# A decoder layer's last attention group: one-column layernorm work moved between engines, work pieces split differently, and other accumulator banks for the last up products

## The chip, the cores and the metric

The kernel runs on one core of a Trainium2 chip. A core has a matrix engine (TensorE, PE in the profile, its weight loads PEld), a vector engine (VectorE, DVE), an activation engine (ScalarE, ACT), a general engine (GpSimd, POOL) and an engine that mostly issues transfers (SyncE, SP). Each engine executes its own instruction stream in order. Transfers are issued by SP and by GpSimd and moved by 16 DMA engines. The metric is the device time of one execution in microseconds, as the median of several runs.

## The reference

One layer of a decoder on x of shape (8, 256, 512), all in float32: attention, a decayed running sum over the context, and a gated feed-forward network, each followed by a layernorm without weights.

```python
x = _layernorm(x + _L0_attn_ref(x, Wq, Wk, Wv, Wo, Wdown, Wup))      # 16 heads of 32
x = _layernorm(x + _L0_xattn_ref(x, ctx_2048, ctx_2048, decay))       # r = d*r + k*v, out = q*r
x = _layernorm(x + _L0_ffn_ref(x, gate_cp, up_cp, down_cp))           # silu(gate)*up, 512 -> 2048 -> 512
return x
```

The three weight matrices of the feed-forward network are spline interpolations of a few thousand control points; the second layernorm sees values of a large range, since its input is x plus x times a running sum.

## The kernel before, in words

The 2048 tokens are four groups (g, 512 tokens) of two sequences each (n = 0 to 7, 256 tokens). PSUM, the matrix engine's accumulator memory, has eight banks: four in the pool `ps_big` and four in `ps_mm`. Every instruction keeps the order in which the Python program writes it, on its engine: the wrapper `Ordered` (line 299) is the helper whose line 308 nearly all rows of the profile carry, so rows are told apart by the names of their tiles.

**Attention loop** (from line 854). There are 32 passes, `s` = 0 to 31, eight to a group: two sequences times four quads of four heads. At the start of pass `s` TensorE makes the scores of pass `s + 1` into the four banks of `ps_big` (`sc`). For each head of the next pass VectorE takes a row maximum (`nmax`) and ScalarE two exponentials (`e`), which frees the head's bank; for each head of this pass TensorE transposes `e` (`tr_e`), an engine copies it out of PSUM (`eT`), and TensorE weights the values with it (`av`). In an odd quad VectorE makes reciprocals of the sums (`rec`) and a copy spread over 512 columns (`wide`, function `divide`), which TensorE transposes (`tr_rec`).

Between these go pieces of other work. Line 836 gives the last group's: for each pass two strings, the first done ahead of the fourth head's transpose, the second behind the fourth head's exponentials. Before each piece in a string, `slot()` advances every open chain by one stage. A piece "o" is two of the four matmuls of an output product (`output`, bank `ps_o`; with the last one VectorE adds `x_t`, the residual rows that `load_rows` fetched); "s" is nothing but the slot; "i" is one of eight pieces of `inputs(b)`, which prepares feed-forward block b. The first four of these transpose a column chunk of `x2` (`tr_x`), copy it to `x2T` and write it to DRAM (`xd`, by a GpSimd transfer issued with the next piece, the fourth with the fifth); the other four are matmuls (`ps_mom`) whose results `mom` go to DRAM (`md`, GpSimd transfers). Windows of `xd` and rows of `md` are read back into `xg` by SP's transfers, which wait for those writes. In the last group `inputs(0)` and `inputs(1)` are made this way.

**Chains.** `norms` runs, a stage per slot, the first layernorm (`norm_plain`), the transpose of the running sum (`tr_r`), `h2`, and the second layernorm, `norm_wide` (lines 381 to 414). Its stages: `nm` and the largest magnitude `mx` on VectorE; then five one-column operations (`mx` limited below by 1, its reciprocal `c`, `nmc`, `ce`, `t`) on VectorE; then ScalarE's square of the row with its sum `ss`, which uses `c` and `nmc`; then `va`, `tt` and `ok` on VectorE with the power `rs` on GpSimd between them; then `rc` and the scaled row, into `x2`, on GpSimd. `recur(n)` fetches a sequence's context, squares it on GpSimd (`r`, 128x1024) and scans it on VectorE.

**Feed-forward blocks** (from line 1115), four of 512 tokens. In each, `gate_up(b, j)` runs for j = 0 to 7: two gate products into two banks of `ps_mm` (`pg`), two up products into two banks of `ps_big` (`pu`), ScalarE's silu (`sg`), VectorE's product (`inter`), and SP's transfer of it, re-sorted, into `nat`. Then `exact(b, t)` for t = 0 to 15 accumulates eight matmul instructions each into four banks of `ps_big` (`y`), which are taken at t = 0; behind t = 0, in blocks 1 to 3, the block before is transposed into four banks of `ps_mm` (`tr_y`). At t = 7 the sums over `nat` are made (`ps_s`), copied and sent by GpSimd's transfers to `fin`, which the last y products of the block (`finish`) read. Behind the gate and up products of a block SP also reads the next block's `xg` and, with the chains, writes `out`.

Of the kernel before, what the change touches and what calls it, by code (L numbers as in the profile page):

```python
# [13 lines left out]
ALU = mybir.AluOpType  # L14
# [3 lines left out]
P = 128  # L18
B, T, D = 8, 256, 512
NH, DH = 16, 32  # L20
# [4 lines left out]
EPS = 1e-5  # L25
# [4 lines left out]
NTILE = INTER // P  # L30
# [285 lines left out]
def decoder_kernel(ctx: ExitStack, tc: tile.TileContext, x, xT, ctxT, wq, wkT, wvT, woT, wdownT, wup, decay, up_taps, down_taps, mom_f, sum_f, out, plan):  # L316
    nc = tc.nc
# [9 lines left out]
    make_identity(nc, ident)  # L327
    neghalf = const.tile([P, 4], F32, name="neghalf")
    nc.gpsimd.memset(neghalf, -0.5)
    x2 = const.tile([P, NT // P, D], F32, name="x2")  # L330


# [10 lines left out]
    early = first.enter_context(tc.tile_pool(name="early", bufs=1, side="right"))  # L343

    nc = Ordered(tc)
    units, chains = [], []

    def slot():

# [31 lines left out]
    def norm_wide(h, s, o):  # L381

        nm = small.tile([P, 1], F32, tag="nm", name="nm")
        nc.vector.tensor_scalar(nm, s, -1.0 / D, None, ALU.mult)
        mx = small.tile([P, 1], F32, tag="mx", name="mx")
        nc.vector.tensor_reduce(mx, h, AX.X, ALU.max, apply_absolute_value=True)
        yield
        nc.vector.tensor_scalar(mx, mx, 1.0, None, ALU.max)  # L390
        c = small.tile([P, 1], F32, tag="c", name="c")
        nc.vector.reciprocal(c, mx)
        nmc = small.tile([P, 1], F32, tag="nmc", name="nmc")
        nc.vector.tensor_tensor(nmc, nm, c, ALU.mult)
        ce = small.tile([P, 1], F32, tag="ce", name="ce")
        nc.vector.tensor_scalar(ce, c, c, EPS, ALU.mult, ALU.mult)
        t = small.tile([P, 1], F32, tag="t", name="t")
        nc.vector.tensor_scalar(t, mx, 2.0**-70, None, ALU.mult)
        yield
        ss = small.tile([P, 1], F32, tag="ss", name="ss")  # L400
        nc.scalar.activation(o, h, AF.Square, bias=nmc, scale=c, accum_out=ss)
        yield
        va = small.tile([P, 1], F32, tag="va", name="va")
        nc.vector.tensor_scalar(va, ss, 1.0 / D, ce, ALU.mult, ALU.add)
        rs = small.tile([P, 1], F32, tag="rs", name="rs")
        nc.gpsimd.tensor_tensor(rs, va, neghalf[:, 0:1], ALU.pow)
        tt = small.tile([P, 1], F32, tag="tt", name="tt")
        nc.vector.tensor_scalar(tt, t, t, ss, ALU.mult, ALU.mult)
        ok = small.tile([P, 1], F32, tag="ok", name="ok")
        nc.vector.tensor_scalar(ok, tt, F32_MAX * 2.0**-140, c, ALU.is_le, ALU.mult)  # L410
        yield
        rc = small.tile([P, 1], F32, tag="rc", name="rc")
        nc.gpsimd.tensor_tensor(rc, rs, ok, ALU.mult)
        nc.gpsimd.tensor_scalar(o, h, nm, rc, ALU.add, ALU.mult)
# [200 lines left out]
    def load_rows(n):  # L615
        xs[n] = []
        for qc in range(2):
            x_t = rows.tile([P, D], F32, tag="row", name="x_t")
            r0 = (n * 2 + qc) * P
            nc.sync.dma_start(out=x_t, in_=x[r0 : r0 + P, :])  # L620
            xs[n].append(x_t)
# [118 lines left out]
    def open_inputs():  # L740
        pool = ctx.enter_context(tc.tile_pool(name="inputs", bufs=1, side="left"))
        ffn["pool"] = pool
        ffn["mom"] = mid.enter_context(tc.tile_pool(name="mom", bufs=1, side="right"))
        ffn["mf"] = pool.tile([P, DC, 2, K2], F32, name="mf")
        nc.sync.dma_start(out=ffn["mf"], in_=mom_f)
# [20 lines left out]
    def inputs(b):  # L766

        pool, mf = ffn["pool"], ffn["mf"]
        xt = pool.tile([P, DC, GT], F32, tag="x2T", name="x2T")
        xd = dram.tile([4 * SPAN, GT], F32, tag="xd", name="xd")  # L770
        md = dram.tile([1, 20 * NTILE, GT], F32, tag="md", name="md")
        xg = pool.tile([P, NTILE // 2, GT], F32, tag="xg", name="xg", bufs=2)
        xgs[b] = xg

        def to_dram(c):
            nc.gpsimd.dma_start(out=xd[c : 4 * (P - 1 - c) + c + 1 : 4, :], in_=xt[c:, c, :])
            if c:
                row = 4 * (SPAN - c) + c - 1
                nc.sync.dma_start(out=xd[row : row + 4 * c - 3 : 4, :], in_=xt[:c, c, :])

        for c in range(DC):
            if c and b < 2:
                to_dram(c - 1)
            tr = ps_mm.tile([P, GT], F32, tag="mm", name="tr_x2")
            for t in range(TC):
                nc.tensor.transpose(tr[:, t * P : (t + 1) * P], x2[:, b * TC + t, c * P : (c + 1) * P], ident)
            (nc.vector.tensor_copy if c % 2 or b < 2 else nc.scalar.copy)(xt[:, c, :], tr)
            if b > 1:
                to_dram(c)
            yield  # L790
        if b < 2:
            to_dram(DC - 1)
        if b > 1:
            reads.append(lambda: windows(xd, xt, xg))
        else:
            windows(xd, xt, xg)
        mo = ffn["mom"].tile([P, ND, GT], F32, tag="fin", name="mom")
        ps = {}
        for c in range(DC):
            for s in (c, c + 1):  # L800
                if s // 2 not in ps:
                    ps[s // 2] = ps_mm.tile([P, GT], F32, tag="mm", name="ps_mom")
                at = slice(s % 2 * K2, (s % 2 + 1) * K2)
                nc.tensor.matmul(
                    ps[s // 2][at, :],
                    lhsT=mf[:, c, s - c, :],
                    rhs=xt[:, c, :],
                    start=(s == c + 1 or c == 0),
                    stop=(s == c or c == DC - 1),
                )  # L810
            if c == 1:
                nc.vector.tensor_copy(mo[:, 0, :], ps[0])
            if c == DC - 1:
                nc.vector.tensor_copy(mo[:, 1, :], ps[1])
                nc.scalar.copy(mo[:K2, 2, :], ps[2][:K2, :])
                nc.gpsimd.dma_start(out=md[:, : 2 * P].rearrange("h (c p) t -> (h p) c t", p=P), in_=mo[:, :2, :])
                nc.gpsimd.dma_start(out=md[0, 2 * P :], in_=mo[:K2, 2, :])
                if b > 1:
                    reads.append(lambda: moments(md, xg))
                else:  # L820
                    moments(md, xg)
            yield
# [10 lines left out]
            ("7k", "3k o o"), ("4k", "1v 2v"), ("6v", "o o 5v"), ("7v", "3v 4v"),  # L833
        ),
    ]
    FILLS = [FILLS[0], FILLS[1], FILLS[1], [("i i", "o o"), ("i i", "s s"), ("i i", "i i"), ("s s", "o o")] * 2]
    outs, ins = [], []

    def fed(g, items, first):
# [14 lines left out]
    for s, (g, bb, quad) in enumerate(steps):  # L854
        n = g * 2 + bb
        feeding = g + 1 < NG
        if quad == 0 and bb == 0:
            if feeding:
                qkvs[g + 1] = group_tiles(g + 1)
                b_now = b_next  # L860
                t_sums = token_sums(b_now, nc.gpsimd, 3 * (g > 1))
                next(t_sums)
                if g < 2:
                    for _ in t_sums:
                        pass
                chains.append(t_sums)
            else:
                first.close()
                open_inputs()
                ins += [inputs(0), inputs(1)]  # L870
        if quad == 0 and n:
            load_rows(n - 1)
            outs += [output(n - 1, qc) for qc in range(2)]
        if n and quad == ((2, 1)[bb] if feeding else 1 + bb):
            chains.append(recur(n))
# [12 lines left out]
        def divide():  # L888
            rec = small.tile([P, 2, 8], F32, tag="rec", name="rec")
            nc.vector.reciprocal(rec, sums[n][:, :, quad // 2 * 8 : quad // 2 * 8 + 8])  # L890
            wide = att.tile([P, 2, 8, DH], F32, tag="wide", name="wide")
            nc.vector.tensor_copy(wide, rec.unsqueeze(3).to_broadcast([P, 2, 8, DH]))
            return wide

        if quad % 2:
# [80 lines left out]
    nc.scalar.activation(neghalf[:, 3:4], neghalf[:, 2:3], AF.Silu)  # L976
    for _ in weights:
        pass
    mid.close()
    load_rows(NG * 2 - 1)  # L980
    units += [["o", output(NG * 2 - 1, qc), DC] for qc in range(2)]
# [9 lines left out]
    def gate_up(b, j):  # L991

        pgs, pus = [], []
        for w, pool, tag, to in ((wg, ps_mm, "mm", pgs), (wu, ps_big, "big", pus)):
            for h in range(2):
                at = slice(h * K2, (h + 1) * K2)
                ps = pool.tile([P, GT], F32, tag=tag, name="pg" if w is wg else "pu")
                nc.tensor.matmul(ps, lhsT=w[at, j * P : (j + 1) * P], rhs=xgs[b][at, j, :], start=True, stop=True)
                to.append(ps)
        for h in range(2):  # L1000
            sg = work.tile([P, GT], F32, tag="sg", name="sg")
            nc.scalar.activation(sg, pgs[h], AF.Silu)
            inter = work.tile([P, GT], F32, tag="inter", name="inter", bufs=NTILE)
            nc.vector.tensor_tensor(inter, pus[h], sg, ALU.mult)
            inters[b, 2 * j + h] = inter
# [196 lines left out]
```

## Time and profile before

| | |
|---|---|
| median of 3 runs | 582.72 us (582.32 to 583.15) |
| the profiled execution | 582.0 us, of which its span is 580.2 us |
| mean granted TensorE clock | 0.993 |
| last attention group (passes 24 to 31) | 308.1 to 380.0 us of the span |
| feed-forward blocks 0, 1, 2, 3 begin (first gate product) | 380.0, 430.0, 478.7, 525.8 us |

| window of the span, 20 us each | PE busy | DVE busy | ACT busy | POOL busy | DMA share |
|---|---|---|---|---|---|
| 320 to 340 | 17.21 | 16.62 | 13.96 | 7.36 | 0.34 |
| 340 to 360 | 18.74 | 14.21 | 13.47 | 4.46 | 0.58 |
| 360 to 380 | 18.48 | 16.81 | 11.90 | 9.52 | 0.61 |
| 440 to 460 | 20.00 | 11.69 | 9.00 | 4.55 | 0.99 |

The profile gives the busy time of each engine, groups of instructions with their mean time, the order in time, and a chain of waits: the work that ended last, followed back at each step to what released it. A row in the order of time reads: start, duration, engine, line, operation, result and inputs, count, and in brackets the time that the engine stood idle before it and what ended that. "x16" on a matrix row counts instructions; a float32 matmul is two.

### The profile page before, as it was taken

Reading aid. Unit: us, or ns where it says so; the run is one execution under the profiler, and the core shown is the slowest. Engines: PE = TensorE matmul, PEld = TensorE weight load, DVE = VectorE, ACT = ScalarE, POOL = GpSimd, SP = SyncE. Lnnn points to the kernel's source line nnn. Section 1 sums busy time; section 2 is a strip of 40 time slices with the busy share of each in tenths; the row PEclk is TensorE's granted clock in tenths of the full one; section 3 lists DMA queues with packets and bytes.
Section 4 is the critical chain, followed back from the end, with each engine's and each line's share of the span. In section 5 each row is a group of like instructions: output and inputs, shape, how many; then the busy total and the mean of one; then the engine's idle time right before and its main releaser. Section 6 shows DMA issues by size and latency. Waiting matters only on the chain.

```text
span 580.2 us, 10416 instructions
## 1 busy us (share of the span) xinstructions
PE 557.7 (96%) x3591; PEld 340.5 (59%) x3591; DVE 342.5 (59%) x742; ACT 273.8 (47%) x821; POOL 283.6 (49%) x583
## 2 busy tenths in 40 slices
PE   9999999999999999999999899899999999999993
PEld 4786777666766776767776455444343444434442
DVE  1336656586686586576587778875436415605615
ACT  0204665556564646654655667663234215305312
POOL 0446368689756648756554413313560362261263
PEclk9999999999999999999999999999999999999997
DMA  8404134333415224325223165689329959985921
GB/s 296 148 0 164 48 111 139 107 109 93 128 41 165 70 73 164 109 64 160 73 73 128 42 148 142 180 169 216 107 88 234 204 174 240 203 233 132 229 101 72
DMA packets 41699, 77.99 MB, mean 134 GB/s; under 512 B 5952, under 2 KB 10448, under 8 KB 41648
## 3 DMA queue, kind: packets, MB, share of 16 engines
q1 hardware_dynamic: 34576, 62.75, 41.5%
q0 software_dynamic: 6064, 13.41, 7.1%
q10 hardware_dynamic: 1008, 1.18, 0.7%
q8 instruction: 28, 0.46, 0.3%
q14 instruction: 23, 0.19, 0.1%
HBM read 45.22 MB, written 11.12 MB: 97 GB/s over the span
## 4 chain that ended last, share of the span: by engine, by line
PE 78%; DVE 8%; DMA 5%; ACT 4%; issue 3%; POOL 1%; SPq 0%; POOLq 0%; DVEq 0%; ACTq 0%
PE y L308 10%; PE ps_k L308 9%; PE ps_q L308 8%; PE ps_o L308 8%; PE ps_v L308 7%; PE tr_e L308 6%; PE pg L308 5%; PE ps_s L308 5%; PE pu L308 5%; PE sc L308 5%; PE av L308 4%; ACT e L308 2%; DMA fin<-sum 2%; DVE nmax L308 2%; DMA x_t<-in_x 1%
## 5 line engine op out<-in xcount | busy, mean ns | idle before, releaser
L308 ACT ACTIVATE e<-sc,nmax 128x256 f32<-128x256 f32 x256 | 120.1, 481 | 94.8 <-DVE nmax L308 94.7
L308 DVE TENSOR_REDUCE nmax<-sc 128x2 f32<-128x512 f32 x128 | 85.1, 682 | 25.9 <-PE sc L308 24.3
L308 POOL TENSOR_TENSOR taps<-taps 128x256 f32<-128x256 f32 (+1 forms) x144 | 86.6, 601 | 13.9 <-DMA taps<-in_down_taps 8.1
L308 PE MATMUL tr_e<-ident,e 128*128 128x128 f32 x512 | 68.4, 276 | 3.1 <-DVE x2T L308 0.9
L308 PEld LDWEIGHTS tr_e<-ident,e 128*128 128x128 f32 x512 | 57.2, 140 | 17.0 <-issue 8.0
L308 PE MATMUL y<-inter,wd 32*128 32x512 f32 x512 | 63.3, 599 | 0.0
L308 PE MATMUL ps_o<-w_o,yT 128*128 128x512 f32 x128 | 58.9, 599 | 1.1 <-DVE q_g L308 0.7
L308 ACT COPY eT<-tr_e 128x512 f32<-128x512 f32 x88 | 51.9, 590 | 17.0 <-PE tr_e L308 17.0
L308 ACT ACTIVATION_READ_ACCUMULATOR e<-sc,nmax 128x1 f32 x256 | 53.4, 209 | 0.0
L308 DVE TENSOR_TENSOR inter<-pu,sg 128x512 f32<-128x512 f32 x64 | 41.2, 686 | 18.7 <-PE pu L308 10.6
L308 POOL TENSOR_SCALAR va<-ss 128x1 f32<-128x1 f32 x32 | 6.3, 198 | 81.3 <-ACT tr_y L308 47.7
L308 ACT ACTIVATE sg<-pg 128x512 f32<-128x512 f32 x64 | 37.2, 597 | 18.5 <-PE pg L308 18.2
L308 PEld LDWEIGHTS y<-inter,wd 32*128 32x128 f32 x512 | 26.6, 184 | 32.4 <-issue 27.4
L308 POOL TENSOR_TENSOR rs<-va,neghalf 128x1 f32<-128x1 f32 x48 | 28.0, 583 | 35.7 <-DVE va L308 33.0
L308 PE MATMUL sc<-k_g,q_g 32*128 32x256 f32 x512 | 40.5, 402 | 0.8 <-ACT e L308 0.4
L308 PEld LDWEIGHTS ps_o<-w_o,yT 128*128 128x128 f32 x128 | 23.0, 190 | 24.8 <-issue 21.0
L308 PE MATMUL av<-eT,v_g 128*32 128x256 f32 x512 | 35.1, 385 | 0.5 <-ACT eT L308 0.5
L308 PEld LDWEIGHTS sc<-k_g,q_g 32*128 32x128 f32 x512 | 25.0, 184 | 16.9 <-issue 11.8
L308 PE MATMUL pg<-xg,wg 64*128 64x512 f32 x128 | 33.4, 599 | 0.0
L308 PE MATMUL pu<-xg,wu 64*128 64x512 f32 x128 | 32.8, 589 | 0.0
L308 POOL COPY x2p<-x 128x4 f32<-128x4 f32 (+4 forms) x144 | 32.7, 278 | 0.0
L308 DVE TENSOR_TENSOR q_g<-ps_q,q_g 128x512 f32<-128x512 f32 x28 | 18.9, 687 | 23.1 <-PE ps_q L308 20.3
(159 smaller groups left out, 915.6 us busy)
## 6 DMA issues: line engine op xcount, KB each, us to landing
nat<-inter SPq DMA_DIRECT2D x64, 256.0 KB
taps<-in_down_taps SPq DMA_DIRECT2D x40, 256.0 KB
taps<-in_up_taps SPq DMA_DIRECT2D x16, 384.0 KB
xg<-xd SPq DMA_DIRECT2D x8, 616.0 KB
r<-in_ctxT SPq DMA_DIRECT2D x8, 512.0 KB
x_t<-in_x SPq DMA_DIRECT2D x16, 256.0 KB
fin<-sum POOLq DMA_DIRECT2D x16, 256.0 KB, 4.8
out<-h SPq DMA_DIRECT2D x16, 256.0 KB
```

What stands on the lines that cost most here:

```text
L308: return lambda *a, **k: self.tc.keep_in_program_order(f(*a, **k))
```

## The change

In the last group and until the attention loop's end a flag `calm` is set. While it is set, the five one-column operations and `va`, `tt` and `ok` of `norm_wide` are issued on GpSimd instead of VectorE; the reciprocal becomes a power of -1, for which a column of constants is filled at the start. `wide` is copied by GpSimd as well. In `inputs(0)` and `inputs(1)` the copy of the fourth chunk to `x2T` is ScalarE's instead of VectorE's. The pieces are split differently around the fourth head: in the second and sixth pass of the last group one of two "i" goes behind it, and in the fourth and eighth pass one of two "o" goes ahead of it. The rows for sequence 6 are fetched at the start of pass 27 instead of 28. In feed-forward blocks 1 to 3 the last pair of up products goes into banks of `ps_mm`, which the gate products use.

```diff
+    nc.gpsimd.memset(neghalf[:, 1:2], -1.0)
...
-    units, chains = [], []
+    units, chains, calm = [], [], [False]
...
-        nc.vector.tensor_scalar(mx, mx, 1.0, None, ALU.max)
+        v = nc.gpsimd if calm[0] else nc.vector
+        v.tensor_scalar(mx, mx, 1.0, None, ALU.max)
         c = small.tile([P, 1], F32, tag="c", name="c")
-        nc.vector.reciprocal(c, mx)
+        if calm[0]:
+            v.tensor_tensor(c, mx, neghalf[:, 1:2], ALU.pow)
+        else:
+            v.reciprocal(c, mx)
...
-        nc.vector.tensor_tensor(nmc, nm, c, ALU.mult)
+        v.tensor_tensor(nmc, nm, c, ALU.mult)
...
-        nc.vector.tensor_scalar(ce, c, c, EPS, ALU.mult, ALU.mult)
+        v.tensor_scalar(ce, c, c, EPS, ALU.mult, ALU.mult)
...
-        nc.vector.tensor_scalar(t, mx, 2.0**-70, None, ALU.mult)
+        v.tensor_scalar(t, mx, 2.0**-70, None, ALU.mult)
...
+        v = nc.gpsimd if calm[0] else nc.vector
         va = small.tile([P, 1], F32, tag="va", name="va")
-        nc.vector.tensor_scalar(va, ss, 1.0 / D, ce, ALU.mult, ALU.add)
+        v.tensor_scalar(va, ss, 1.0 / D, ce, ALU.mult, ALU.add)
...
-        nc.vector.tensor_scalar(tt, t, t, ss, ALU.mult, ALU.mult)
+        v.tensor_scalar(tt, t, t, ss, ALU.mult, ALU.mult)
...
-        nc.vector.tensor_scalar(ok, tt, F32_MAX * 2.0**-140, c, ALU.is_le, ALU.mult)
+        v.tensor_scalar(ok, tt, F32_MAX * 2.0**-140, c, ALU.is_le, ALU.mult)
...
-            (nc.vector.tensor_copy if c % 2 or b < 2 else nc.scalar.copy)(xt[:, c, :], tr)
+            (nc.vector.tensor_copy if (c < 3 if b < 2 else c % 2) else nc.scalar.copy)(xt[:, c, :], tr)
...
-    FILLS = [FILLS[0], FILLS[1], FILLS[1], [("i i", "o o"), ("i i", "s s"), ("i i", "i i"), ("s s", "o o")] * 2]
+    FILLS = [FILLS[0], FILLS[1], FILLS[1], [("i i", "o o"), ("i", "i s s"), ("i i", "i i"), ("s o", "s o")] * 2]
...
+                calm[0] = True
                 ins += [inputs(0), inputs(1)]
+        if n and quad == 0 and s < 28 or s == 27:
+            load_rows(n if s == 27 else n - 1)
         if quad == 0 and n:
-            load_rows(n - 1)
...
-            nc.vector.tensor_copy(wide, rec.unsqueeze(3).to_broadcast([P, 2, 8, DH]))
+            (nc.gpsimd if calm[0] else nc.vector).tensor_copy(wide, rec.unsqueeze(3).to_broadcast([P, 2, 8, DH]))
...
+    calm[0] = False
     mid.close()
...
-        for w, pool, tag, to in ((wg, ps_mm, "mm", pgs), (wu, ps_big, "big", pus)):
+        up = (ps_mm, "mm") if b and j == NTILE // 2 - 1 else (ps_big, "big")
+        for w, pool, tag, to in ((wg, ps_mm, "mm", pgs), (wu, *up, pus)):
```

## The prediction

> **What bounds the kernel now.** I read the page first: TensorE is busy in nearly every slice, so only work or waits in front of TensorE count.
>
> ```profile
> PE 557.7 (96%) x3591; PEld 340.5 (59%) x3591; DVE 342.5 (59%) x742; ACT 273.8 (47%) x821; POOL 283.6 (49%) x583
> ```
>
> Next, the timeline of the last group, 308.1 to 380.0 us. I number its eight loop passes 24 to 31; a pass begins with the score matmuls (sc) of the next one: 308.13, 317.67, 325.66, 335.92, 345.04, 354.26, 361.90, and 371.97 for the last, which has none. VectorE is the busiest engine beside TensorE (60.2 of 76 us from 308 to 384, in the table of windows), and it queues the one-column work in front of the maxima that ScalarE's exponentials wait for. Three times in passes 25 to 30 it even stands still for ScalarE's square:
>
> ```profile
> 323.49 0.21 DVE L308 TENSOR_SCALAR va<-ss,ce 128x1 f32<-128x1 f32 x1 [0.60 <-ACT x L308]
> ...
> 342.60 0.21 DVE L308 TENSOR_SCALAR va<-ss,ce 128x1 f32<-128x1 f32 x1 [1.26 <-ACT x L308]
> ...
> 368.87 0.21 DVE L308 TENSOR_SCALAR va<-ss,ce 128x1 f32<-128x1 f32 x1 [1.88 <-ACT x L308]
> ```
>
> Third, the chain of waits over that stretch. Half of it is no engine at all: a transfer waits for a transfer, and VectorE for the last.
>
> ```profile
> 339.38 6.23 DMA md<-mom
> ...
> 347.44 7.54 DMA x_t<-in_x
> ...
> 355.11 0.33 DVE h L308
> ```
>
> Last, the same chain in feed-forward block 1; blocks 2 and 3 look alike. The first eight y matmuls take 2.55 us where eight take 1.07 in block 0: they need the banks of the last up products. Later TensorE waits for the sums to come back by DMA.
>
> ```profile
> 446.92 0.86 PE pu L308 x4
> 447.78 2.55 PE y L308 x8
> ...
> 458.45 7.04 PE ps_s L308 x32
> ...
> 466.50 6.70 DMA fin<-sum
> ...
> 473.34 3.67 PE y L308 x8
> ```
>
> **The change, part by part: the attention stretch.** Four second layernorms pass through it. Each takes mx, c, nmc, ce, t off VectorE (336.44 to 337.14: 0.7 us) and va, tt, ok (308.07 to 308.71: 0.65 us). Four copies to wide (0.426 each) and two of eight x2T copies (0.68) leave it too, and the three waits above go (3.7 us). That is 4x1.35 + 1.7 + 1.4 + 3.7 = 12.2 us of VectorE time, but little of it is TensorE's time, so I go pass by pass.
>
> Costs on GpSimd: a 128x1 operation there takes 0.19 to 0.21 us (va 0.198, rc 0.214), the power 0.56 (rs). The first five cost 4x0.2 + 0.56 + gaps = 1.6 us, va, rs, tt, ok 1.4 us. wide is not shown on GpSimd: its ends are 0.32 (copy of 128x80) and 1.27 (two-input 128x512); I take 0.85, near the one-input 128x512 at 0.77 to 0.82. [...]
>
> *Pass 24*: nothing. *Pass 25*: only one x2T copy stands before the third maximum, no wide, no va. The fourth maximum is done at 324.0 instead of 325.92. ScalarE now bounds: square to 323.35, eT 0.6, four exponentials 1.82: 325.8 instead of 327.08. Gain 1.3. The ScalarE copy of the fourth x2T column (0.586) falls after them, into 1.8 us of idle. *Pass 26*: TensorE works back to back (328.40 to 335.92), the 1.3 stays; VectorE, full from 328 on, drops 0.7 more, so its second mom copy ends 2.0 earlier (336.4). *Pass 27*: TensorE waits there until 338.38 for that copy and until 339.58 for an eT; the first half of the output product (1.73 us) fills this, delays the fourth transpose, but its eT stands behind ScalarE's square anyway. Exponentials end near 343.0, TensorE's work at 343.4 (now 345.04, then stalled): the next transposes start 2.4 earlier. *Pass 28*: VectorE waits for x_t. Moving load_rows saves nothing by itself: on SP's queue no other instruction lies between the end of pass 26 and the start of pass 28, so x_t stays behind xg<-md, which waits for md. md starts 2.0 earlier with mom, but GpSimd's longer queue (wide, then va, tt, ok ahead of r*r, 1.89 us) sends the last xd at 330.3 instead of 329.50, and xg<-xd shares the DMA engines with md. I take x_t 1.6 earlier (ends 0 and 2.0): the gain falls to 1.6. *Pass 29*: as 25, without square and va: 0.8 more, 2.4. *Pass 30*: back to back again; the x2T copy on ScalarE delays a bank by 0.4, the 0.53 us wait for h goes: 2.5. *Pass 31*: of waits of 0.56, 0.27 and what surrounds them (the 16 transposes take 3.24 us, 1.75 of them work) the half product fills about 0.9: 3.4 us at the first gate product.
>
> Covers. The squares need nmc from GpSimd: it is ready 4.7 us before in pass 25, 4 in 27, 2 in 30, and about 1.2 late in 31, where only eT of the last head is queued behind the square, 1.5 us before its use. If the cover of 27 or 30 went, two exponential pairs behind the square would wait and each microsecond would show. wide is needed by tr_rec, 1 to 2 us later in 25 and 27, level with it in 29 and 31: 0.5 us at most there.
>
> **What comes of it in block 0.** ps_s begins at 410.52 and needs the last nat at 411.4; DMA traffic dies off by 410.0, at about 212 GB/s without a break before. So 1.4 us is slack. The stream starts when SP passes md of block 1 (378.38). There GpSimd's queue is the tightest: va to ok, rc, the 0.77 us scaling, r*r, the five, two md issues; I put md 2.4 earlier on issue but, with xg<-xd 1.6 later beside it, 1.3 earlier on landing (ends 0 and 2.4). So 1.4 + 1.3 = 2.7 of the 3.4 us pass. Ends 1.4 and 3.4.
>
> **The seams.** The last up products now wait for the silu of the pair before: done at 446.42, needed at 446.76: no wait, 0.3 us to spare (upper end 0.3 each). The four y banks are free at 447.44 against 447.71: 1.48 us goes (2.55 less 1.07). tr_y wants banks at 448.8 to 450.1; silu and inter free them at 447.5 to 449.16. In block 3 this reaches the end, but nat traffic stops at 549.8 and would be needed just then: I take 1.3 (ends 0.9, 1.48). In blocks 1 and 2 TensorE then waits for fin: its four transfers land 7.9 us after issue, against 2.3 in blocks 0 and 3, because 2.4 MB on SP's queue (xg, out) are ahead until about 468.4; 1 MB at 250 GB/s after that gives 472.6, and it landed at 473.2. Nothing of that moves with the seam. I take 0.2 each (ends 0, 1.48). [...] The added memset (0.1 us) lies on idle GpSimd time at the start.
>
> **Sum.** 2.7 + 0.2 + 0.2 + 1.3 = 4.4 us. The profiled execution took 582.0 (span 580.2 and 1.8 around it): 577.6. It lies 0.7 below the median 582.72, so 578.3 as a median.
>
> **Rivals.**
> *Transfers hold it* (0.18): x_t and md land when they do now. Then pass 29 starts afresh, block 0 lets only its 1.4 us slack through, and block 3 gives 1.3: 2.7 us, 580.0. For it: the chain above; against it: md follows mom.
> *The seam's wait only moves* (0.08), to tr_y or to the up products: 2.7 us of attention alone, 580.0. Against it: the bank times above.
> *Nothing holds it* (0.13): 3.4 + 0.4 (x_t at its other end) + 3x1.48 = 8.2, 574.5. Against it: nat and fin backlogs.
> *Slower: GpSimd's queue becomes the bound* (0.15). Place: passes 30 and 31, where r*r, eight one-column operations, the md issues and wide stand in one queue, and ScalarE's square and SP's md wait on it. It decides once md of block 1 is issued later than 374.36 + 1.4 + 1.3 = 377.1, the slack and block 3's gain being used up; each microsecond beyond costs one. If each of the 14 new operations in 29 to 31 took 0.56 as the power does, that is 14x0.36 = 5.0 us more than I reckon; on top of 372.0, with the square that much later once (1.6), md is issued at 378.6, 1.5 past the point: 584.2. Against it: 128x1 rows of 0.2, and GpSimd at 9.5 of 20 us from 360 to 380.
>
> **Numbers.** My forecast has 0.46 and its own range 576.5 to 579.7 (block 0 at its ends, 1.4 and 3.4, and 1 us more for fin below). A measurement of this kernel can tell about 0.2% (1.2 us) from no change: faster is below 581.5, slower above 583.9. Of the two 580.0 cases (0.26) I leave 0.09 within that bound, because their waits can also grow. Faster 0.46 + 0.13 + 0.17 = 0.76, same 0.09, slower 0.15. The range 574.5 to 583.5 leaves out most of the slower case and the lower half of the case without a hold.
>
> **What would show it.** Right: DVE's waits for ACT x gone between 317 and 380, exponentials of pass 25 ending near 325.8, y x8 at 1.1 us in blocks 1 to 3, and a longer wait of y for fin in blocks 1 and 2 (about 2 us where now 0.79 and 1.00). The first gate product near 376.6; ps_s of block 0 interrupted or late against it. Wrong: ACT waiting for POOL nmc in passes 27 or 30, PE waiting for wide, x_t landing at 355 or later, tr_y or pu waiting for banks. The forecast fails as a whole if md of block 1 is issued later than now.

## The result, and the profile after

| | before | after |
|---|---|---|
| median, runs side by side | 582.93 us (582.32 to 584.05) | 589.64 us (588.41 to 590.32) |
| ratio after to before, 95% interval | | 1.0111 (1.0086 to 1.0135) |
| the profiled execution, its span | 582.0, 580.2 us | 588.4, 586.6 us |
| mean granted TensorE clock | 0.993 | 0.985 |
| first gate product of blocks 0, 1, 2, 3 | 380.0, 430.0, 478.7, 525.8 us | 381.9, 438.1, 486.6, 532.4 us |

The change costs 6.7 us; 578.3 was forecast. Executions of one kernel spread by some 6 us (the kernel before took 582.14 to 588.07 us in one series of 25), so smaller differences below are read from the intervals and from places in the traces. The two traces also start the last group 0.39 us apart (second pass at 317.67 before, 317.28 after); where I say "aligned", that is taken out.

The page of the kernel after, engine totals and the granted clock by slices:

```profile
PE 556.5 (95%) x3591; PEld 343.2 (59%) x3591; DVE 334.5 (57%) x704; ACT 274.2 (47%) x823; POOL 297.0 (51%) x620
...
PEclk9999999999999999999999997999899999999997
```

VectorE lost 8 us of work and GpSimd got 13.4 more. New is a TensorE clock that falls in two places, slices 25 (352 to 367 us) and 29 (411 to 425 us).

The chain of waits of the kernel after (start, duration, what):

```profile
337.82 8.80 DMA md<-mom
...
348.46 8.53 DMA x_t<-in_x
...
379.11 5.92 DMA md<-mom
...
408.40 9.11 DMA nat<-inter
...
417.75 7.92 PE ps_s L308 x28
```

Against the chain before, md of block 1 and nat of block 0 are new in it (and, behind these lines, nat of block 3). The order in time of the kernel after, where these transfers hold the engines:

```profile
357.12 0.69 DVE L308 SCALAR_TENSOR_TENSOR h<-ps_o,x_t 128x512 f32<-128x512 f32 x1 [7.42 <-DMA x_t<-in_x]
...
357.87 1.11 PE L308 MATMUL tr_e<-ident,e 128*128 128x128 f32 x4 [3.96 <-DVE h L308]
...
385.34 1.09 ACT L308 ACTIVATE sg<-pg 128x512 f32<-128x512 f32 x2 [2.20 <-DMA md<-mom]
...
417.75 7.92 PE L308 MATMUL ps_s<-nat,sf 128*64 128x512 f32 x28 [3.16 <-DMA nat<-inter]
```

VectorE waits 7.42 us for x_t (2.56 before), TensorE stands still for 3.96, and then four transposes take 1.11 us where they took 0.60 to 0.66. The first silu waits 2.20 us for md; I take it that `sg` lies in memory that `mom` held until its transfer was done. The sums of block 0 wait for nat, and 28 of their instructions take 7.92 us (32 took 7.02 before). The table of windows of the kernel after shows why both are slow. A row gives the window and its length, the busy time of PE, PEld, DVE, ACT and POOL with the number of instructions, and then the granted clock, the DMA share and GB/s:

```profile
350.00:355.00 5.00, 3.91 (x42) 2.00 (x40) 0.00 (x0) 1.89 (x7) 0.76 (x1) 1.00 0.83 181
355.00:360.00 5.00, 2.04 (x9) 1.64 (x10) 2.88 (x6) 1.02 (x4) 0.00 (x0) 0.70 0.17 55
360.00:365.00 5.00, 5.00 (x41) 3.98 (x43) 3.63 (x10) 4.66 (x17) 2.19 (x5) 0.62 0.48 131
...
418.00:421.00 3.00, 3.00 (x10) 1.07 (x8) 0.00 (x0) 0.58 (x1) 0.68 (x1) 0.57 0.00 0
```

With each of the two waits the clock is granted at half (0.50): from 357.0 (before the wait ends) to 363.8, and from 418.5 to 421.9 us, read in steps of 0.2 us.

Where the waits come from is on the queues. GpSimd's order in time, after:

```profile
321.44 0.61 POOL L308 COPY wide<-rec 128x512 f32<-128x512 f32 x1 [3.72 <-DVE nm L308]
...
323.25 0.26 POOL L308 TENSOR_SCALAR va<-ss,ce 128x1 f32<-128x1 f32 x1 [0.60 <-ACT x L308]
...
329.51 1.21 POOL L308 TENSOR_SCALAR x<-h,nm,rs 128x512 f32<-128x512 f32 x1
330.67 0.62 POOL L308 DMA_DIRECT2D xd<-x2T  x1
...
340.61 0.26 POOL L308 TENSOR_SCALAR va<-ss,ce 128x1 f32<-128x1 f32 x1 [1.13 <-ACT x L308]
...
367.92 0.63 POOL L308 DMA_DIRECT2D xd<-x2T  x1
```

The last row is from pass 30; before, that column stood here:

```profile
362.04 0.62 POOL L308 DMA_DIRECT2D xd<-x2T  x1
```

The wait of `va` for ScalarE's square has not gone with the move; it stands on GpSimd now, 0.60, 1.13 and in pass 30 2.46 us, and there transfers are queued behind it. The last column of block 0 is sent at 330.67 (329.50 before), that of block 1 at 367.92 (362.04). SP's order in time, after, shows what follows:

```profile
333.56 1.53 SPq L308 DMA_DIRECT2D xg<-xd  x4
346.69 1.73 SPq L308 DMA_DIRECT2D xg<-md  x2
348.46 0.96 SPq L308 DMA_DIRECT2D x_t<-in_x  x2
...
370.82 1.54 SPq L308 DMA_DIRECT2D xg<-xd  x4
385.10 1.57 SPq L308 DMA_DIRECT2D xg<-md  x2
...
388.27 12.04 SPq L308 DMA_DIRECT2D nat<-inter  x9
```

Before, these six stood at 332.37, 345.68, 347.44, 365.11, 378.38 and 382.84; the first two:

```profile
332.37 1.53 SPq L308 DMA_DIRECT2D xg<-xd  x4
345.68 1.72 SPq L308 DMA_DIRECT2D xg<-md  x2
```

`xg<-md` waits until md has landed (9.4 us behind its issue, after). GpSimd issues md of block 0 earlier than before (336.96 against 338.62), yet it lands later: about 13 us behind the windows xg<-xd in both kernels. The traces of the runs below agree: 12.7 us (late_rows) to 14.6 us (late_norm_dve) in block 0, whether md was issued 3.3 us (late_b1) or 7.8 us (best_c) behind the windows. x_t waits behind md on SP's queue, and so do `sf` (the constants of the sums) and nat in block 0.

Aligned ledger: the transposes of pass 28 begin 2.5 us earlier than before, pass 30 3.1 us later (x_t, half clock), the first gate product 2.3 later, block 1 8.5 later (nat, half clock); the seams (the passages from a block's last up products to its first y products) and the rest of blocks 1, 2 and 3 give back 0.22, 1.31 and 0.33. At the last products (`ps_c`) that is 6.6 us. The half clock alone I estimate at 4.4 of them: six groups of four transposes at about 1.06 instead of 0.60 (2.7), and 7.92 against the 6.23 us that the same 28 instructions take at full clock in runs below (1.7).

The seam in block 1, chain of the kernel after:

```profile
455.00 0.86 PE pu L308 x4
455.86 1.07 PE y L308 x8
...
473.10 7.96 DMA fin<-sum
```

The 2.55 us are 1.07, as forecast, and the sums come back 7.96 us after their issue, so most of it is waited again: y waits 2.06 us for fin (0.79 before).

### The profile page after: what moved, and what is told of

Same layout as the page of the kernel before. It is cut to its first block, busy times and chain, and to the rows that moved or that the text cites. A ratio compares the mean times of both kernels' runs of the same rounds, so it can differ in the third digit from the quotient of the medians.

```text
span 586.6 us, 10419 instructions
## 1 busy us (share of the span) xinstructions
PE 556.5 (95%) x3591; PEld 343.2 (59%) x3591; DVE 334.5 (57%) x704; ACT 274.2 (47%) x823; POOL 297.0 (51%) x620
## 3 DMA queue, kind: packets, MB, share of 16 engines
q10 hardware_dynamic: 1008, 1.18, 0.6%
## 4 chain that ended last, share of the span: by engine, by line
PE 77%; DMA 10%; DVE 6%; ACT 3%; issue 2%; POOL 1%; SPq 0%; POOLq 0%; ACTq 0%; DVEq 0%
PE ps_k L308 9%; PE ps_q L308 8%; PE ps_v L308 8%; PE tr_e L308 7%; PE ps_o L308 7%; PE y L308 7%; PE sc L308 5%; PE ps_s L308 5%; PE pg L308 5%; PE av L308 5%; PE pu L308 4%; DMA nat<-inter 3%; DMA fin<-sum 3%; DMA md<-mom 3%; ACT e L308 2%; PE ps_mom L308 2%
## 5 line engine op out<-in xcount | busy, mean ns | idle before, releaser
L308 PE MATMUL y<-inter,wd 32*128 32x512 f32 x512 | 58.9, 599 | 0.0
L308 PEld LDWEIGHTS y<-inter,wd 32*128 32x128 f32 x512 | 24.9, 184 | 29.7 <-issue 27.4
L308 PE MATMUL sc<-k_g,q_g 32*128 32x256 f32 x512 | 38.9, 401 | 0.4 <-ACT e L308 0.2
L308 PE MATMUL pg<-xg,wg 64*128 64x512 f32 x128 | 36.4, 600 | 0.3 <-ACT sg L308 0.3
L308 PE MATMUL pu<-xg,wu 64*128 64x512 f32 x128 | 35.7, 589 | 0.0
L308 PE MATMUL ps_s<-nat,sf 128*64 128x512 f32 x128 | 30.5, 626 | 4.1 <-DMA nat<-inter 4.1
```

The costliest lines, as they stand in the source:

```text
L308: return lambda *a, **k: self.tc.keep_in_program_order(f(*a, **k))
```

## The experiments

Theory 1 was: GpSimd's queue sends the last column late, with it go the windows, md, x_t, the first silu and nat. Theory 2: the results that GpSimd now makes (nmc, wide) are late for ScalarE and TensorE. Theory 3: the seam's banks. All runs are timed beside the kernel before; a table stands at the end.

**Each half of the change alone.** seam_only is the kernel before with

```diff
-        for w, pool, tag, to in ((wg, ps_mm, "mm", pgs), (wu, ps_big, "big", pus)):
+        up = (ps_mm, "mm") if b and j == NTILE // 2 - 1 else (ps_big, "big")
+        for w, pool, tag, to in ((wg, ps_mm, "mm", pgs), (wu, *up, pus)):
```

> The kernel before, with nothing but the last up products of blocks 1 to 3 in the banks of the gate products. Theory 1 (the whole loss comes from the attention stretch: GpSimd's queue sends the last x2T column later, and with it the transfers that follow): the three waits of y at the seam go, 2.55 to 1.07 us each, block 2 (its carry of 1.3 in the changed kernel) keeps most of it and blocks 1 and 3 give theirs back to the sums and the rows that come by DMA: 581.0 to 582.5, no more than 0.3 above the kernel before. Theory 3 (the banks cost more than they bring, because up products now wait for the silu of the pair before): 584 or more, and 'pu' waiting for ACT.

attn_only is the changed kernel with these lines as before.

> The changed kernel with the last up products left in their old banks, so the attention stretch alone is changed. Theory 1: the first block 1 gate product stands 8 us later than in the kernel before, as in the changed kernel (438.14 against 430.06), and the end 7 to 8 us later than before: 590 to 591. Theory 3 (the banks are what costs): 583 to 584.

582.07 and 590.61 us: the whole loss lies in the attention stretch. Theory 3 falls.

**The column sent at once, and x_t ahead of md.** xd_now, on the changed kernel:

```diff
-            if c and b < 2:
-                to_dram(c - 1)
...
-            if b > 1:
-                to_dram(c)
+            to_dram(c)
             yield
-        if b < 2:
-            to_dram(DC - 1)
```

> The changed kernel, but each x2T column of inputs 0 and 1 is sent as soon as it is copied, not with the next piece. Theory 1: SP issues xg<-xd of block 0 at about 330 instead of 333.56 and that of block 1 3 to 5 us earlier than 370.82; md lands 13 us behind each, so the wait of VectorE for x_t in pass 28 falls from 7.4 us to about 4, and the first silu and the nat stream come 3 to 5 us earlier: 584 to 586 in all. Theory 2 (GpSimd's late results, nmc and wide, hold ScalarE and TensorE, and the transfers only follow): 589 to 590. Theory 3 (the banks): 589 to 590.

rows_26:

```diff
-        if n and quad == 0 and s < 28 or s == 27:
-            load_rows(n if s == 27 else n - 1)
+        if n and quad == 0 and s < 28 or s == 26:
+            load_rows(n if s == 26 else n - 1)
```

> The changed kernel, but load_rows(6) is issued at the start of pass 26, not 27, so on SP's queue x_t stands ahead of xg<-md of block 0, not behind it. Theory 1: the 7.4 us wait of VectorE for x_t in pass 28 is gone, pass 29 starts 4 us or more earlier; the second half of the delay (xg<-xd of block 1, then md, then nat) shrinks by less, since it follows GpSimd's queue: 584 to 587. Theory 2 (nmc and wide late) and theory 3 (banks): 589 to 590.

584.79 and 585.07 us, some 5 us better each, as theory 1 had it; theory 2 gave 589 to 590. In xd_now the last columns go at 327.16 and 362.68, xg<-xd at 330.03 and 366.48, x_t is waited for 1.90 us and nat starts at 382.60. This profiled execution, 581.19 us, is the shortest of ten; the four above 586 us had a mean clock of 0.987 to 0.990, this one 0.993. In rows_26 that wait is gone and the first gate product comes 3.6 us earlier than before (aligned), but nat still starts at 383.78 (382.9 aligned, against 382.84 before), and in the profiled execution TensorE waits 3.41 us for it, with the half clock behind.

**Which part makes the queue late.** Each run undoes one part of the changed kernel: norm_dve issues the eight one-column operations on VectorE again, wide_dve the copy to `wide`, pieces_old has the old strings and the fourth column's copy on VectorE.

```diff
-        v = nc.gpsimd if calm[0] else nc.vector
+        v = nc.vector
```

> The changed kernel, with the eight one-column operations of each second layernorm back on VectorE; wide stays on GpSimd, the pieces stay split. Theory 1a (these operations are what makes GpSimd's queue send the last column late): in block 0's turn va, tt, ok (0.3 each with gaps 1.2 us) leave the queue, in block 1's turn mx to t (1.9 us): last xd near 329.5 and 364.5 instead of 330.67 and 367.92, x_t 1.2 us earlier, nat 3 us earlier: 585 to 587. Theory 1b (wide on GpSimd does it) or 1c (the split of the pieces does it): 589 to 590.

```diff
-            (nc.gpsimd if calm[0] else nc.vector).tensor_copy(wide, rec.unsqueeze(3).to_broadcast([P, 2, 8, DH]))
+            nc.vector.tensor_copy(wide, rec.unsqueeze(3).to_broadcast([P, 2, 8, DH]))
```

> The changed kernel, with the copy to wide back on VectorE alone. Theory 1a or 1c: 588.5 to 590, since wide lies 0.6 us ahead of an xd that is followed by a wait for ScalarE anyway. Theory 1b: 584 to 586, last xd of block 1 at 365 or earlier.

```diff
-    FILLS = [FILLS[0], FILLS[1], FILLS[1], [("i i", "o o"), ("i", "i s s"), ("i i", "i i"), ("s o", "s o")] * 2]
+    FILLS = [FILLS[0], FILLS[1], FILLS[1], [("i i", "o o"), ("i i", "s s"), ("i i", "i i"), ("s s", "o o")] * 2]
```

> The changed kernel, with the pieces ordered as before the change and the fourth x2T column copied by VectorE. Theory 1c (the later place of the second piece and of the copy is what sends the columns late): 584 to 586, last xd at 329.5 and 364 or earlier. Theory 1a or 1b: the last xd stays where it is within 0.5 us, since r*r and the layernorm's operations still stand before it, and TensorE loses the gain of pass 25: 589 to 591.

585.58, 588.45 and 588.28 us. The one-column operations are the main part: with them on VectorE the last columns go at 330.03 and 364.40, and x_t is waited for 4.41 us instead of 7.42. From norm_dve:

```profile
355.48 0.69 DVE L308 SCALAR_TENSOR_TENSOR h<-ps_o,x_t 128x512 f32<-128x512 f32 x1 [4.41 <-DMA x_t<-in_x]
...
364.40 0.62 POOL L308 DMA_DIRECT2D xd<-x2T  x1
```

wide does little. The pieces lie between what theories 1a and 1c gave: the last column of block 1 goes 2 us earlier with the old order (365.88 against 367.92), so they have a small share.

**The kernel before with the rows early** (the edit of rows_26 on the kernel before):

> The kernel before, with nothing but load_rows(6) at the start of pass 26, ahead of the transfers that wait for md. Theory 1 (the rows stand behind md on SP's queue in both kernels): VectorE's wait of 2.56 us for x_t in pass 28 goes, pass 30 and with it the last xd of block 1, md and nat come up to 2.5 us earlier: 580 to 581.5. If the place on SP's queue is not what holds x_t: 582.5 to 583.5, wait still there.

584.13 us, ratio 1.0014 (0.9992 to 1.0035): a miss for both. The wait for x_t is gone, and pass 30 begins at 361.81 against 361.90 us. The 2.56 us that VectorE stood still before were covered: TensorE waits for an x2T copy in both, 0.95 us before and 1.18 here, and goes on at the same time:

```profile
359.44 0.66 PE L308 MATMUL tr_e<-ident,e 128*128 128x128 f32 x4 [1.18 <-DVE x2T L308]
```

The tail of a chain of waits is no proof that its link costs time.

**The half clock.** warm puts three products without use ahead of the sums of block 0 in the changed kernel:

```diff
+                if b == 0:
+                    warm = ps_mm.tile([P, GT], F32, tag="mm", name="warm")
+                    for _ in range(3):
+                        nc.tensor.matmul(warm, lhsT=wd[:, :P], rhs=inters[b, t], start=True, stop=True)
```

> The changed kernel, with three extra matrix products (2.8 us by y's 0.46 us an instruction; the result is not used) on TensorE just ahead of the sums of block 0, where it waits 3.16 us for the last nat and then runs its 28 sum instructions at a granted clock near 0.5 (7.92 us instead of 6.23). Theory 4 (a TensorE wait of some 2.4 us and more makes the clock fall to half for some 3.3 us, which adds 1.7 us behind the wait): the wait shrinks under 1 us, the sums take 6.23, and 1.0 to 1.7 us go: 588 to 588.6. Rival (the sums are slow because nat arrives piece by piece): still 7.9 us, no gain, 589.6 or more.

Order in time of warm:

```profile
412.84 2.84 PE L308 MATMUL warm<-inter,wd 128*128 128x512 f32 x6
415.62 1.08 PE L308 MATMUL ps_s<-nat,sf 128*64 128x512 f32 x4
417.26 6.23 PE L308 MATMUL ps_s<-nat,sf 128*64 128x512 f32 x28 [0.56 <-DMA nat<-inter]
```

588.09 us: more work on TensorE, and by the medians 1.5 us less (ratio 1.0059 against 1.0111; the two intervals touch). The same 28 instructions take 6.23 us when TensorE did not stand still ahead of them, though they too wait for the last nat, 0.56 us, and start only 0.5 us earlier than in the kernel after (417.26 against 417.75). Not all of the gain is theirs: in this trace the half clock of pass 28 also lasts 3.4 us instead of 6.8, and pass 30 begins 0.9 us earlier (aligned). The 2.4 us of theory 4 is no bound on which these traces agree: the half clock followed a wait of 2.35 us in rows_26 and not one of 2.87 us in wide_dve.

**Transfers off GpSimd's queue.** best_a is the changed kernel with the edit of rows_26 and

```diff
-            nc.gpsimd.dma_start(out=xd[c : 4 * (P - 1 - c) + c + 1 : 4, :], in_=xt[c:, c, :])
+            (nc.gpsimd if b > 1 else nc.sync).dma_start(out=xd[c : 4 * (P - 1 - c) + c + 1 : 4, :], in_=xt[c:, c, :])
...
-                if b > 1:
+                if b:
                     reads.append(lambda: moments(md, xg))
```

and each column sent with its own piece. best_b has the one-column operations on VectorE besides; best_c is the kernel before with the seam and this diff.

> The changed kernel with its transfers taken off GpSimd's queue and off each other: both parts of each x2T column of blocks 0 and 1 are issued by SP right behind the copy, load_rows(6) comes in pass 26, and xg<-md of block 1 is issued behind block 0's nat. Theory 1: xg<-xd of block 0 at 330 or earlier, no wait for x_t, pass 30 at 360 to 361, first nat at 380 to 381.5 instead of 388.27, block 0's sums 2 us earlier than in the kernel before, and the seam's 1: 578.5 to 580.5. Theory 2 (nmc and wide late hold the engines): 583 or more, since their waits in pass 31 (1.86 and 1.5 us) stay.

> As the run before, with the one-column operations of the second layernorm back on VectorE (wide on GpSimd, pieces split). Theory 1: the transfers no longer depend on GpSimd's queue, so these operations matter little now: within 1 us of the run before, 578.5 to 581. Theory 2: 2 us or more better than the run before, ACT's wait for nmc in pass 31 being gone.

> The kernel before, with the last up products in the gate products' banks, both parts of each x2T column of blocks 0 and 1 issued by SP right behind the copy, and xg<-md of block 1 behind block 0's nat; nothing of the layernorm, wide, pieces or rows is moved. Theory 1: xg<-xd of block 0 at 328 to 330, of block 1 at 361 to 363, first nat near 381.5, and 1 to 1.5 us from block 0 and 1 from the seams: 580 to 581.5; what best_a has beyond it is what the moved work brings once the transfers don't wait for it.

580.59, 582.0 and 581.9 us, with ratios of 0.9957, 0.9957 and 0.9961: all faster than before, but each 0.1 to 1 us above its expected range. On SP's queue the last column of block 1 lies right behind r (512 KB), and the windows of block 1 are issued at 367.74 in best_a and 369.02 in best_c (365.11 before), 5.2 and 7.2 us behind that column (3.1 before); md lands behind them: SP passes it, with `sf`, at 382.23 and 384.81, and TensorE waits 1.63 and 1.52 us for the first silu (0.35 in the kernel after). A hold was moved, not taken away. The one-column operations make no difference between best_a and best_b that these runs can tell.

**Both holds apart.** Two holds are left: on SP's queue x_t stands behind md, and md lands behind the windows. Blocks 2 and 3 read their windows and rows behind nat. late_b1 lets block 1 do so too, on the changed kernel:

```diff
-        if b > 1:
+        if b:
             reads.append(lambda: windows(xd, xt, xg))
...
-                if b > 1:
+                if b:
                     reads.append(lambda: moments(md, xg))
```

> The changed kernel, but block 1's windows (xg<-xd) and rows (xg<-md) are read behind block 0's nat transfers, as blocks 2 and 3 do it, instead of in passes 30 and 31. If the windows in flight are what holds md: md of block 1 lands 5 to 7 us behind its own issue (near 384 or earlier), the first silu waits 1 us or less for it, the first nat goes at 383.5 to 384.5 instead of 388.27, and since fewer bytes share the DMA engines with nat the sums of block 0 wait less than 1 us: 584 to 585.5. The wait for x_t in pass 28 (7.4 us) and the half clock behind it stay. If md is late for itself: nat at 387 or later, 588 to 589.

late_rows has this and the edit of rows_26.

> As the run before, and load_rows(6) in pass 26, so both holds are gone. If the two holds carry the whole loss, the forecast of the attention stretch and of the seam comes true: first gate product 3.4 us earlier than in the kernel before (near 376.6 on its time axis), first nat at 379 to 380, no wait of the sums over 1 us, block 1 begins 3 us or more earlier than in the kernel before, the seams give another 1: 577 to 579. If something else in the moved work costs time: 581 or more.

late_before is the kernel before with the seam and this diff.

> The kernel before with the seam's banks and with block 1's windows and rows read behind block 0's nat; nothing of the layernorm, wide, pieces or rows moved. Its first gate product stays at 380.0 and its first silu waits for nothing, so nat starts at 382.5 to 383 as before and has fewer bytes beside it: block 0 gives 0 to 0.5 us, the seams 1: 581 to 582. What late_rows has beyond it is what the moved work brings when no transfer holds it, about 3 us; if it has less than 1 us more, the moved work brings nothing.

584.65 and 578.05 us lie in their ranges, 582.09 lies 0.09 above its own. In late_b1 md is issued at 379.10, and `sf`, which waits for it on SP's queue, goes at 383.25, 4.1 us later instead of 6.8:

```profile
379.10 1.42 POOL L308 DMA_DIRECT2D md<-mom  x2
...
383.25 0.33 SPq L308 DMA_DIRECT2D sf<-in_sum_f  x1
```

nat starts at 385.57, 1 us later than expected, and the sums are not interrupted; the wait for x_t (7.81 us) and the half clock behind it remain. late_rows, the chain of waits:

```profile
376.91 1.06 PE pg L308 x4
...
407.39 7.02 PE ps_s L308 x32
...
426.86 1.06 PE pg L308 x4
...
461.88 8.28 DMA fin<-sum
...
536.64 9.55 DMA nat<-inter
...
560.29 2.87 PE ps_c L308 x12
```

The first gate product and block 1 come 3.7 us earlier than before (aligned by 0.48), the last products (`ps_c`) 4.8. The clock stays at full. late_rows is 0.97% faster than the kernel before (0.9903, 0.9874 to 0.9932); late_before 0.36%. The difference, 0.6% or some 4 us, is what the moved work brings once no transfer waits for it. The early rows are counted with it; alone, on the kernel before, they brought nothing (before_rows_26). The waits of theory 2 in pass 31 are still there in late_rows (1.86 us for nmc, 1.48 for `wide`), so they are not what made the change slower.

**Which part brings the gain.** late_norm_dve and late_pieces are late_rows with the edits of norm_dve and pieces_old.

> late_rows with the one-column operations of the second layernorm back on VectorE. If they bring most of the gain of the attention stretch, VectorE waits again for ScalarE's square (1.7 us in pass 27, 1.9 in pass 31), the first gate product comes 2 us later than in late_rows and the kernel takes 580 to 581. If they bring little: within 0.7 us of late_rows, 577.5 to 579.

> late_rows with the order of the pieces and the fourth column's copy as before the change. If the split brings most of the gain (the prediction: TensorE's 1.3 us in pass 25 and what lies after the fourth head in 27 and 31): first gate product 1.5 to 2.5 us later than in late_rows, 579.5 to 581. If it brings little: 577.5 to 579.

578.67 and 580.08 us. Each part is worth about 1 us at the first gate product (377.4 and 377.3 against 376.4, aligned), less than the 2 expected of the operations and the 1.5 to 2.5 of the pieces. The time of late_pieces does lie where the pieces would bring most of the gain. Their ratios, 0.9923 (0.9905 to 0.994) and 0.9942 (0.9927 to 0.9956), overlap with that of late_rows, so the shares at the end stay open.

| run | median us | ratio to before | 95% interval |
|---|---|---|---|
| seam_only | 582.07 | 0.9982 | 0.9952 to 1.0012 |
| attn_only | 590.61 | 1.0132 | 1.0088 to 1.0176 |
| xd_now | 584.79 | 1.0023 | 0.9997 to 1.0048 |
| rows_26 | 585.07 | 1.0025 | 1.0003 to 1.0047 |
| norm_dve | 585.58 | 1.0038 | 1.0009 to 1.0067 |
| wide_dve | 588.45 | 1.0096 | 1.0059 to 1.0133 |
| pieces_old | 588.28 | 1.0086 | 1.0061 to 1.0112 |
| before_rows_26 | 584.13 | 1.0014 | 0.9992 to 1.0035 |
| warm | 588.09 | 1.0059 | 1.0031 to 1.0088 |
| best_a, best_b, best_c | 580.59, 582.0, 581.9 | 0.9957, 0.9957, 0.9961 | 0.9931 to 0.9983 at the widest |
| late_b1 | 584.65 | 1.0030 | 1.0007 to 1.0054 |
| late_rows | 578.05 | 0.9903 | 0.9874 to 0.9932 |
| late_before | 582.09 | 0.9964 | 0.9944 to 0.9985 |
| late_norm_dve | 578.67 | 0.9923 | 0.9905 to 0.9940 |
| late_pieces | 580.08 | 0.9942 | 0.9927 to 0.9956 |

## Why the prediction was wrong, point by point

**The step that failed** is that of pass 28: "I take x_t 1.6 earlier (ends 0 and 2.0)". x_t came 2.4 us later (aligned). The step had all the parts: x_t behind xg<-md, md behind GpSimd's queue, the last xd later (0.8 forecast, 1.6 measured, aligned), the windows beside md. But it took md's landing from md's issue, which did come earlier, and let the windows only shave it. The runs show the reverse: with the windows in flight md lands when the traffic dies off (DMA share 0.52 from 345 to 346 us and 0.01 in the next, after), 12.7 to 14.6 us behind the windows' issue in block 0, and SP passes it 4.1 us behind its own issue when they are away (block 1 of late_b1 and late_rows). An earlier md then buys nothing, and a later last column costs. Why the smaller transfer waits for the larger ones, no run shows. That the end of the range was 0 and not a loss is the same fault.

**The same step once more, in block 0.** "1.3 earlier on landing (ends 0 and 2.4)" for md of block 1 was 7.1 us later (aligned), since the pass itself began 3.1 late and GpSimd's queue added the rest: the last column went at 367.92 instead of 362.04. 1.4 us of slack could not hold that. The prediction had named this as what makes it fail as a whole: md of block 1 issued later than before, 378.25 against 374.36.

**A term that is not in the sum.** The clock of TensorE. By the estimate above the half clock behind the two long waits makes 4.4 of the 6.6 us.

**The slower rival** had the right engine and queue and was priced too low, at 584.2. It looked for the price where ScalarE and SP wait in passes 30 and 31; the queue did its harm first in passes 25 and 26, through a transfer several links ahead of the wait. And it had "each microsecond beyond costs one", while the clock was at half behind both waits of 3 to 4 us.

**A wait that was moved was counted as gone.** "The three waits above go (3.7 us)": they went from VectorE to GpSimd (0.60, 1.13, 2.46 us), whose queue sends the columns.

**Pass 28 as a bound before.** The prediction read VectorE's 2.56 us wait for x_t as what holds the pass. before_rows_26 shows that it held nothing; the room it left was small, and the change used it up.

**Costs and covers, mostly too small.** Costs on GpSimd: `va` 0.26, `tt` and `ok` 0.32 against 0.2 forecast, `wide` 0.61 against 0.85, the power 0.56 to 0.83 against 0.56; the first five of a layernorm 1.8 us in pass 25 and 2.4 in pass 27 instead of 1.6. nmc in pass 31 was 1.86 us late against 1.2, wide 1.48 against 0.5 at most.

**What was right.** Passes 25 to 27: the transposes of pass 28 begin 2.5 us earlier (2.4 forecast, aligned). The first gate product "near 376.6" came in late_rows at 376.4, and all of the 3.7 us passed through block 0, where 2.7 of 3.4 were forecast, as nat there starts right behind the first products (379.63), with xg<-md behind it (402.93) and no longer ahead of it (378.38 before). The seams: 1.07 us instead of 2.55 at once; carried were 0.22, 1.31 and 0.33 in blocks 1, 2, 3 against 0.2, 0.2 and 1.3, so the sum (1.9 against 1.7) was right and the places were not: in block 3 the sums wait 0.95 us for nat. That the sum agrees is luck. The forecast of 578.3 us is the time of late_rows, not of the change as it was made, and there too the parts differ: 3.7 us up to block 1 and 1.1 behind it, where 2.7 and 1.7 were forecast.

## What to carry to other kernels

When work is moved to an engine that also issues transfers, follow every transfer that is queued behind it, to the last wait that hangs on it, and take a transfer's landing from all that is in flight beside it, not from its own issue. Work that waits can keep its wait on the new engine (here `va`, 0.60 to 2.46 us), and holds there what stands behind it. Before a link of a chain is priced, ask what else would end last without it; and count more than its length for a long wait of TensorE: in these traces each of 3.16 us and more brought a stretch at half clock.

## What the runs showed of the hardware that was not expected

- **The clock behind a wait.** The granted clock was 0.50 for 6.8 us after a TensorE wait of 3.96 us and for 3.4 us after one of 3.16 us (after), for 6.8 us after 4.36 us (late_b1) and for 3.4 us after 3.74 us (warm). In attn_only, wide_dve and rows_26 (3.29, 3.25 and 3.41 us) the 28 sum instructions behind the wait took 7.92 us instead of 6.23, and in wide_dve four transposes behind a wait of 3.66 us took 1.12 us. Of shorter waits, one of 2.35 us (rows_26, eight y instructions in 5.37 us instead of 3.67) and one of 2.56 us (pieces_old, the sums in 7.89 us) were followed by it too, others of 2.06 (after), 2.32 (best_b), 2.36 (late_rows) and 2.87 us (wide_dve) were not. Of the executions of the kernel before in the series of late_rows, three of the four above 586 us had a mean clock of 0.988, the others 0.991 or more.
- **A small transfer behind large ones.** With the windows (xg<-xd, four transfers, two each of 616 and 88 KB) in flight md (two transfers, 512 and 128 KB) lands up to 9.4 us (after) or 10.4 us (rows_26) behind its issue. With none in flight (block 1 of late_b1) SP passes both 4.1 us behind the first one's issue; the shortest landing in that trace is 3.2 us.
- **Sending from another queue.** The last column, sent by GpSimd, let SP go on 3.1 us after its issue (362.04 to 365.11, before); sent by SP behind r it took 7.2 us (361.82 to 369.02, best_c) and 5.2 us (best_a). That r is what held it was not tried.
